# Folding one column of a projection into the stage beside it, and a margin in a list scheduler: a four-layer graph network on one core

## The chip, the cores and the metric

The kernel runs on one core of a Trainium2 chip. The metric is device time in microseconds (us) of one execution; lower is better. Engines are named as in the profile: PE is TensorE (PEld its weight loads), DVE is VectorE, ACT is ScalarE, POOL is GpSimd, SP issues DMAs.

## What is computed

Inputs are `x` (64 graphs, 256 nodes, 128 features, float32) and one weighted adjacency `adj` (256 x 256). Four layers follow each other, each a layer norm, a relu and a graph block whose output is added to `x`:

```
h = relu(layernorm(x)); x = x + GRU(h, adj)          # 5 gated steps, each mixing nodes with adj
h = relu(layernorm(x)); x = x + cheb(h, adj)         # relu([h, A h, 2 A A h - h] @ Theta + bias)
h = relu(layernorm(x)); x = x + conv(h, adj)         # row-normalised ((A h + h) @ W + bias)
h = relu(layernorm(x)); x = x + attention(h, adj)
```

In the attention block, with `W = adj` (256 x 256) cut into two halves of 128 columns, and `E = 256` features:

```
s1 = x @ W[:, :F].T ; s2 = x @ W[:, F:].T            # [B, 256, 256]
pre[i, j, e] = s1[i, e] + s2[j, e] + b_lin[e]
score[i, j] = sum_e leaky_relu(pre[i, j, e]) * a[e] + bias[i, j]
out = sigmoid(softmax_j(score) @ x)
```

The sum over `e` for every pair (i, j) is by far the largest part: 64 x 256 x 256 x 256 elements pass through a min or a relu.

## The kernel before, in words

**Pairs.** Two graphs make a pair; 32 pairs are worked on one after the other. A *front* (`front(p)`) computes the first three layers of pair p and the operands of its attention. *Tiles* make the pairwise elements, *scores* add them up on PE, and a *tail* (`tail`) does softmax, the weighted sum and the store for 128 nodes i of the pair.

**Tiles.** The features are sorted by the sign of `a`, so that two features of equal sign share one pass. A pair has 64 slots of two halves. A relu tile `rl` is 128 x 2048 float32 and belongs to one half of one slot: DVE makes it with one `min` (L854), ACT with eight relu activations (L868), POOL with eight min operations (L876). Three of ten slots are joined: POOL issues a DMA that adds one tile onto the other (L893), so PE sees one tile for two. Thirteen tile buffers circulate; a buffer comes free when PE has scored it or when the DMA has landed.

**Scores.** For a tile PE issues four matmuls of 128x32 weights by 512 columns into one bank (L935), side by side in the four column groups of the array (`side_by_side`, L395 to L398).

**The odd feature.** When one feature has no partner, its contribution is computed apart. In the front, after hT is made, `g2` (128x32; its column 0 gives the linear term, column 1 the s2 term of the odd feature, the rest is zero) is multiplied with four quarters of hT, 128 tokens each, into four partition groups of one bank (L686). Between these, hT's quarter itself is the stationary operand and `w1_odd` (one column) the moving one (L688): that gives the odd feature's s1 with tokens on partitions. ACT copies the bank to `quarter` (L692) and adds the bias into `s1o` (L694). Two DMAs write rows 0 and 1 of each partition group to DRAM (`row`, L699), and one reads them back, broadcast to all partitions (`rows`, L702). The tail uses them at L739 (DVE, with `s1o` as pointer scalar) and L749 (POOL).

**Order.** The order of every engine's instructions is fixed when the kernel is built. A planner keeps a clock for each engine. Fronts, tails and constants are generators which yield the engine of their next step and the time at which its operands are ready; `ran(engine, us, *after)` books the step with a cost written into the code (`PROJECT, MIX, TURN, ...` at L448; 0.6 for the odd stage on PE). `chain_ready(key, e)` returns when a chain's next step may start on an engine. Of what is ready, tails come before fronts, and fronts before tiles and scores; on PE, scores come first when at most one tile buffer is free. Fronts start up to two pairs ahead and are held back by a due count (`STEPS_OF_FRONT`, `SPREAD`, `AHEAD`). Dependencies keep each engine in this order. The planner's times never reach the chip: only the order does, and each engine waits for what an instruction really needs.

The chain of a gated step: mix (PE) -> copy mT (ACT) -> two products (PE) -> tanh (ACT) -> rh (DVE) -> products (PE) -> tanh d (ACT, L561) -> subtract (POOL, L565) -> L568, L572 (DVE, makes hT) -> turn (PE, L426: four 128x128 transposes) -> copy h (ACT, L584) -> the next mix.

Of the kernel before, what the change touches and what calls it, by code (L numbers as in the profile page):

```python
# [8 lines left out]
F32 = mybir.dt.float32  # L9
AF = mybir.ActivationFunctionType  # L10
OP = mybir.AluOpType
# [3 lines left out]
P = 128  # L15
NB = 2
# [6 lines left out]
PE, DVE, ACT, POOL = ENGINES = (mybir.EngineType.PE, mybir.EngineType.DVE, mybir.EngineType.Activation, mybir.EngineType.Pool)  # L23
SLOTS = 64
SHARE = (3, 10)
AHEAD_OF = 2
LOW = 1
ISSUE, ADDED, LANDED, SLACK = 0.65, 5.3, 6.6, 0.3


@with_exitstack
def kernel(
# [50 lines left out]
    nc = tc.nc  # L83
    B, N, D = x.shape
    NC = N // P
    NPAIR = B // NB
# [3 lines left out]
    const = ctx.enter_context(tc.tile_pool(name="const", bufs=1))  # L90
    work = ctx.enter_context(tc.tile_pool(name="work", bufs=2))
# [14 lines left out]
    def ran(engine, us, *after):  # L106
        start = max(clock[engine], 0.0, *after)
        if engine == ACT:
            behind[0] = max(0.0, behind[0] - (start - clock[ACT])) + 0.024 * us
        clock[engine] = start + us  # L110
        return clock[engine] + SEEN[engine] + (behind[0] if engine == ACT else 0.0)

    def moved(since):

        queue[0] = max(queue[0], since) + 0.5
        return queue[0] + 2.2

    spare = [[b, 0.0] for b in banks[5:]]

    def take():  # L120

        spare.sort(key=lambda b: b[1])
        return spare.pop(0)
# [86 lines left out]
    win_n = const.tile([P, 63], F32, name="win_n")  # L210
    w1 = const.tile([P, N], F32, name="w1")
    w2n = const.tile([P, N], F32, name="w2n")
    odd_one = const.tile([P, 34], F32, name="odd_one")
    g2, w1_odd, b_odd = odd_one[:, 0:32], odd_one[:, 32:33], odd_one[:, 33:34]
    blin_s = const.tile([P, NE], F32, name="blin_s")
    SET_UP = set()

# [44 lines left out]
    def other_constants():  # L262
# [5 lines left out]
        t = ran(DVE, 0.8)  # L268

        for c in range(NC):  # L270
            yield PE, t, 1
            b = take()
            for k in range(NC):
                nc.tensor.matmul(b[0][:, 0:N], adj_t[:, k, c * P:(c + 1) * P], adj_n[:, k, :], start=(k == 0), stop=(k == NC - 1))
            t = ran(PE, 1.2, t, b[1])
            yield DVE, t
            nc.vector.tensor_scalar(adj_2[:, c, :], b[0][:, 0:N], 2.0, None, op0=OP.mult)
            t = ran(DVE, 0.35, t)
# [22 lines left out]
        t = ran(DVE, 1.5)  # L301
        yield PE, t, 1
        b = take()
# [5 lines left out]
        t = ran(PE, 0.6, t, b[1])  # L309
        yield DVE, t  # L310
        nc.vector.tensor_copy(columns(14, 3), b[0][:, 0:3])
        t = ran(DVE, 0.1, t)
# [27 lines left out]
        t = ran(DVE, 1.6)  # L340
# [11 lines left out]
        for c in range(NC):  # L352
            yield PE, t, 1
            b = take()
            for k in range(NE):
                nc.tensor.matmul(b[0][:, 0:N], adj_s[:, k, c * P:(c + 1) * P], moved_to[:, k].rearrange("p h m -> p (h m)"),
                                 start=(k == 0), stop=(k == NE - 1))
            t = ran(PE, 1.2, t, b[1])
# [5 lines left out]
            t = ran(DVE, 0.35, t)  # L364
# [3 lines left out]
        b = take()  # L368
# [8 lines left out]
        t = ran(PE, 1.4, t_in, b[1])  # L377
        yield DVE, t
        nc.vector.tensor_copy(blin_s, b[0][:, 1:4:2])
        nc.vector.tensor_copy(odd_one, b[0][:, 4:38])  # L380
        nc.vector.memset(win, 0.0)
        nc.vector.memset(win_n, 0.0)
        nc.vector.tensor_copy(win[:, 31:32], b[0][:, 0:1])
        nc.vector.tensor_scalar(win_n[:, 31:32], b[0][:, 0:1], -1.0, None, op0=OP.mult)
        t = ran(DVE, 0.7, t)
        spare.append([b[0], t])
        SET_UP.add("all")

# [11 lines left out]
    def flat(t):  # L400
        return t.rearrange("p b n -> p (b n)")
# [43 lines left out]
    SHORT = dict(tag="short", bufs=12)  # L445


    PROJECT, MIX, TURN, PRODUCT, PRODUCTS = 0.86, 1.74, 0.69, 0.88, 2.64  # L448
    COPY, BIASED, TANH, ELEMENTS = 0.48, 0.58, 0.57, 0.61

    def norm(src, since, h):

        stats = work.tile([P, NB * NC, 3], F32, name="stats")
        mv = work.tile([P, NB * NC, 2], F32, name="mv")
        s, h = rows_of(src), rows_of(h)[:, :, 0:D]
        yield DVE, since
        for k in range(0, NB * NC, 2):
            nc.vector.bn_stats(stats[:, k:k + 2, :].rearrange("p k s -> p (k s)"), s[:, k:k + 2, :].rearrange("p k d -> p d k"))
        t = ran(DVE, 0.8, since)
        yield POOL, t  # L460
        inverse_root(mv[:, :, 1], stats[:, :, 2], 1.0 / D, OP.mult, LN_EPS, OP.add)
        t = ran(POOL, 1.45, t)
        yield DVE, t
        nc.vector.scalar_tensor_tensor(mv[:, :, 0], stats[:, :, 1], -1.0, mv[:, :, 1], op0=OP.mult, op1=OP.mult)  # L464
        t = ran(DVE, 0.1, t)
        yield ACT, t
        for k in range(NB * NC):
            nc.scalar.activation(h[:, k, :], s[:, k, :], AF.Relu, bias=mv[:, k, 0:1], scale=mv[:, k, 1:2])  # L468
        return ran(ACT, 1.55, t)

    def copied(name, bank, t):

        c = feat(name, **(SHORT if name not in KEPT else KEPT[name]))
        nc.scalar.copy(c, by_feature(bank[0]))  # L474
        t = ran(ACT, COPY, t)
        spare.append([bank[0], t])
        return c, t
# [5 lines left out]
    def front(p):  # L483
# [8 lines left out]
        t = yield from norm(x0, 20.0 if p else 3.0, h)  # L492
        yield PE, t, 1
        b = take()
        to_feature(b[0], h)
        t_h = t
        t = ran(PE, TURN, t, b[1])
        yield ACT, t
        hT, t_hT = copied("hT", b, t)
        for step in range(STEPS):  # L500
            yield PE, t_h, 1, lambda: "adj" in SET_UP
            b = take()
            mix_nodes(b[0], h, adj_t)
            t = ran(PE, MIX, t_h, b[1])
            yield ACT, t
            mT, t_m = copied("mT", b, t)
            if p == 0:
# [6 lines left out]
                t = ran(PE, PROJECT, t_m)  # L514
# [3 lines left out]
            else:  # L518
# [4 lines left out]
                t = ran(PE, 2 * PROJECT, t_m, t_hT, pr[1])  # L523
# [3 lines left out]
            t = ran(ACT, TANH, t, r[1])  # L527
# [4 lines left out]
            if p == 0:  # L532
# [5 lines left out]
                t = ran(PE, PROJECT, t_rh)  # L538
            else:
# [7 lines left out]
                t = ran(PE, 2 * PROJECT, t_rh, pv[1])  # L547
# [6 lines left out]
            if p < 1:  # L554
                nc.scalar.activation(pv[0], pv[0], AF.Tanh, bias=bh, scale=1.0)
                t = ran(ACT, TANH, t)
                yield DVE, t
                nc.vector.tensor_sub(d, by_feature(pv[0]), hT)
                t = ran(DVE, ELEMENTS, t)
            else:  # L560
                nc.scalar.activation(d, by_feature(pv[0]), AF.Tanh, bias=bh, scale=1.0)  # L561
                t = ran(ACT, TANH, t)
# [3 lines left out]
                t = ran(POOL, 1.3, t)  # L566
            yield DVE, max(t, t_z)
            nc.vector.scalar_tensor_tensor(by_feature(pr[0]), by_feature(pr[0]), 1.0, d, op0=OP.add, op1=OP.mult)  # L568
            t = ran(DVE, ELEMENTS, t, t_z)
# [3 lines left out]
            hT = hT_new  # L573
            t_hT = ran(DVE, ELEMENTS)
# [3 lines left out]
            b = take()  # L578
            to_token(b[0], hT)
            t = ran(PE, TURN, t_hT, b[1])  # L580
# [9 lines left out]
        t = ran(DVE, ELEMENTS, t)  # L590
# [6 lines left out]
        b = take()  # L597
        mix_nodes(b[0], h, adj_n)
        t = ran(PE, MIX, t_h, b[1])
# [3 lines left out]
        b = take()  # L603
        to_feature(b[0], h)
        t = ran(PE, TURN, t_h, b[1])
        yield ACT, t
        hT, t = copied("hT", b, t)
        yield PE, t_h, 1
        b = take()
        mix_nodes(b[0], h, adj_2)  # L610
        t = ran(PE, MIX, t_h, b[1])
        yield ACT, t
        c2T, t = copied("c2T", b, t)
# [3 lines left out]
        t = ran(PE, PRODUCTS, t, po[1])  # L617
# [3 lines left out]
        t = ran(DVE, ELEMENTS, t)  # L621
# [3 lines left out]
        t = ran(DVE, ELEMENTS)  # L625
# [4 lines left out]
        t = yield from norm(x2, t, h)  # L630
        yield PE, t, 1
        b = take()
        mix_nodes(b[0], h, adj_ti)
        t = ran(PE, MIX, t, b[1])
        yield ACT, t
        yT, t = copied("yT", b, t)
# [3 lines left out]
        t = ran(PE, PRODUCT, t, po[1])  # L640
# [3 lines left out]
        t = ran(DVE, ELEMENTS, t)  # L644
# [3 lines left out]
        t = ran(ACT, COPY, t)  # L648
# [3 lines left out]
        t = ran(DVE, ELEMENTS, t)  # L652
        yield POOL, t
        inverse_root(rn, rn, MOST_POSITIVE, OP.min, NORM_EPS * NORM_EPS, OP.max)
        t = ran(POOL, 1.35, t)
# [3 lines left out]
        for k in range(NB * NC):  # L659
            nc.vector.scalar_tensor_tensor(rows_of(x3)[:, k], pt[:, k], rn[:, k:k + 1], rows_of(x2)[:, k],  # L660
                                           op0=OP.mult, op1=OP.add)
        t = ran(DVE, 1.04, t)
# [5 lines left out]
        t = yield from norm(x3, t, h3)  # L668
        yield PE, t, 1
        b = take()  # L670
        to_feature(b[0], h3)
        t = ran(PE, TURN, t, b[1])
        yield ACT, t
        hT, t_hT = copied("hT3", b, t)
# [7 lines left out]
        t_s2a = ran(ACT, COPY, t_s2a)  # L682
        yield PE, t_hT, 1
        b = take()
        for g in range(4):
            nc.tensor.matmul(b[0][g * 32:(g + 1) * 32, 0:P], g2, flat(hT)[:, g * P:(g + 1) * P],  # L686
                             start=True, stop=True, skip_group_check=True)
            nc.tensor.matmul(b[0][:, P + g:P + g + 1], flat(hT)[:, g * P:(g + 1) * P], w1_odd, start=True, stop=True)  # L688
        t = ran(PE, 0.6, t_hT, b[1])
        yield ACT, t  # L690
        quarter = work.tile([P, P], F32, name="quarter", bufs=1)
        nc.scalar.copy(quarter, b[0][:, 0:P])  # L692
        s1o = work.tile([P, NB * NC], F32, name="s1o")
        nc.scalar.activation(s1o, b[0][:, P:P + NB * NC], AF.Identity, bias=b_odd, scale=1.0)  # L694
        t = ran(ACT, 0.35, t)
        spare.append([b[0], t])
        row = dram.tile([2, NB * N], F32, name="row", bufs=2)
        for k in range(2):
            nc.sync.dma_start(row[k].rearrange("(q n) -> q n", q=4), quarter[k:P:32, :])  # L699
            t = moved(t) if k else max(t, moved(t) - 2.2)  # L700
        rows = work.tile([P, 2, NB, N], F32, name="rows")
        nc.sync.dma_start(rows.rearrange("p k b n -> p (k b n)"), row.rearrange("k t -> (k t)").unsqueeze(0).to_broadcast([P, 2 * NB * N]))  # L702
# [1 line left out]
        t = moved(t) + 1.5  # L704
        t_lin = t
        yield PE, t_hT, 1
        b = take()
        project(b[0], w2n[:, P:2 * P], hT)
        t = ran(PE, PROJECT, t_hT, b[1])
# [3 lines left out]
        b = take()  # L713
        project(b[0], w1[:, P:2 * P], hT)
        t = ran(PE, PROJECT, t_hT, b[1])
# [6 lines left out]
        b = take()  # L722
        project(b[0], w1[:, 0:P], hT)
        t = ran(PE, PROJECT, t_hT, b[1])
# [235 lines left out]
    def chain_ready(key, e):  # L960

        engine, since, bank, gate = (*CHAINS[key][1], 0, None)[:4] if len(CHAINS[key][1]) < 4 else CHAINS[key][1]
        if engine != e or bank and not spare or gate and not gate():
            return None
        if not isinstance(key, tuple) and 0 < key < NPAIR and spare:

            due = STEPS_OF_FRONT * (scored[0] / (2 * SLOTS) - (key - 2)) / SPREAD
            if CHAINS[key][2] > due + AHEAD:
                return None
        return max(since, min(b[1] for b in spare)) if bank else since  # L970

    def advance(key):
        chain = CHAINS[key]
# [12 lines left out]
    while scored[0] < 2 * NSLOT or CHAINS:  # L986
        while begun_fronts[0] < NPAIR and begun_fronts[0] < 2 + (scored[0] + 2 * SLOTS - 1) // (2 * SLOTS):
            begin_front()
        e = min(now, key=now.get)
        todo = []  # L990
        for key in CHAINS:
            since = chain_ready(key, e)
# [6 lines left out]
        else:  # L999
            since = tile_ready(e)  # L1000
# [6 lines left out]
        if ready:  # L1007
            if e == PE and len(tiles) <= LOW:
                ready = [x for x in ready if x[1] == (2,)] or ready
# [45 lines left out]
```

## Time and profile before

| what | us |
|---|---|
| median of three runs (lowest, highest) | 4951.56 (4950.31, 4957.7) |
| the profiled execution | 4965.92 |
| its span | 4964.1 |
| L854 DVE tiles, 1813 | 4057.4 busy |
| L868 ACT tile parts, 10128 | 4045.6 busy |
| L876 POOL tile parts, 6256 and 1880 | 2962.8 and 899.2 busy |
| L893 POOL issues of adding DMAs, 614 | 575.6 busy |
| L935 PE scores, 27856 records | 2198.3 and 1322.4 busy |
| L686 and L688 PE, 256 records each | 52.1 and 49.8 busy |
| granted PE clock, mean | 0.993 of full speed |

How to read it: a matmul of float32 leaves two records. Matmuls are pipelined, so the distance between the starts of groups, not the length of a record, is what a group costs PE; a score group of eight records starts every 0.86 us. The first 125 us hold the constants and the fronts of pairs 0 and 1; the last front ends at about 4791 us, and from there the engines drain.

### The profile page before, as it was taken

To read this page: it belongs to the slowest core of one execution; us is meant where nothing else is said; L and a number is where in the kernel's file an instruction comes from. 1 tells how busy PE (TensorE), PEld (TensorE's weight loads), DVE (VectorE), ACT (ScalarE), POOL (GpSimd) and SP (SyncE) were. 2 spreads that over 40 slices of the span, in tenths; PEclk is the share of its full clock that TensorE was granted. 3 is DMA by queue.
4 is the path that set the end of the run, shared out by engine and by line. 5 is a ranking of instruction groups with operands and counts; after the bars stand their busy time and mean duration, and the time that the engine had idled before them with its cause. 6 is when DMAs were issued, how large, how long until landed. Compare 5 with 4: busy or idle time off the path is not lost.

```text
span 4964.1 us, 133991 instructions
## 1 busy us (share of the span) xinstructions
PE 4840.3 (98%) x52487; PEld 1793.6 (36%) x52487; DVE 4663.4 (94%) x3288; ACT 4672.1 (94%) x12177; POOL 4684.9 (94%) x9454
## 2 busy tenths in 40 slices
PE   8999999999999999999999999999999999999987
PEld 3333333333333333333333333333333333333322
DVE  3899999999999999999999999999999999999998
ACT  3999999999999999999999999999999999999998
POOL 1899999999999999999999999999999999999998
PEclk9999999999999999999999999999999999999999
DMA  0577667667667676666776676767667767767677
GB/s 18 115 149 145 140 137 148 138 144 150 131 140 147 138 152 138 142 139 135 151 146 139 142 144 132 145 143 144 137 140 145 145 137 143 144 132 144 142 155 145
DMA packets 132363, 687.44 MB, mean 138 GB/s; under 512 B 14096, under 2 KB 49040, under 8 KB 53136
## 3 DMA queue, kind: packets, MB, share of 16 engines
q0 software_dynamic: 88416, 643.86, 64.7%
q1 hardware_dynamic: 42592, 35.01, 2.4%
q8 instruction: 410, 6.72, 0.5%
q14 instruction: 225, 1.84, 0.1%
q10 hardware_dynamic: 720, 0.00, 0.0%
HBM read 26.48 MB, written 8.52 MB: 7 GB/s over the span
## 4 chain that ended last, share of the span: by engine, by line
PE 58%; POOL 11%; DVE 8%; DMA 4%; ACT 4%; issue 3%; POOLq 0%; DVEq 0%; ACTq 0%
PE bank L935 36%; PE bank L398 18%; POOL rl L876 8%; DVE rl L854 6%; DMA rl<-rl 4%; ACT rl L868 3%; PE bank L426 2%; POOL rl L893 1%; PE bank L688 1%; PE bank L686 1%; PE bank L419 1%; POOL d L565 1%; DVE mv L464 0%; POOL mv L393 0%; DVE hT L572 0%
## 5 line engine op out<-in xcount | busy, mean ns | idle before, releaser
L854 DVE TENSOR_TENSOR rl<-s1a,bank 128x2048 f32<-128x2048 f32 x1813 | 4057.4, 2278 | 132.2 <-PE bank L935 70.2
L868 ACT ACTIVATE rl<-bank,s1b 128x256 f32<-128x256 f32 x10128 | 4045.6, 773 | 98.6 <-PE bank L935 57.6
L876 POOL TENSOR_SCALAR rl<-s2n,s1b 128x256 f32<-128x256 f32 x6256 | 2962.8, 669 | 65.0 <-PE bank L935 21.4
L935 PE MATMUL bank<-rl,win_n 128*32 128x512 f32 x17728 | 2198.3, 595 | 56.6 <-DVE rl L854 29.7
L935 PE MATMUL bank<-rl,win 128*32 128x512 f32 x10128 | 1322.4, 594 | 0.0
L935 PEld LDWEIGHTS bank<-rl,win_n 128*32 128x32 f32 x17728 | 555.1, 110 | 1220.6 <-issue 984.5
L876 POOL TENSOR_SCALAR rl<-s2c,s1a 128x256 f32<-128x256 f32 x1880 | 899.2, 658 | 13.6 <-PE bank L935 5.2
L893 POOL DMA_DIRECT2D rl<-rl x614 | 575.6, 949 | 12.5 <-DVE rl L854 6.8
L935 PEld LDWEIGHTS bank<-rl,win 128*32 128x32 f32 x10128 | 324.2, 110 | 653.4 <-issue 535.8
L398 PE MATMUL bank<-mT,wts 128*32 128x512 f32 x2560 | 337.3, 596 | 1.2 <-DVE rh L530 1.1
L398 PE MATMUL bank<-adj_t,h 128*32 128x256 f32 x5120 | 311.8, 383 | 4.8 <-ACT h L584 4.8
L565 POOL TENSOR_TENSOR d<-d,hT 128x512 f32<-128x512 f32 x155 | 227.3, 1466 | 70.0 <-ACT d L561 69.9
L398 PEld LDWEIGHTS bank<-adj_t,h 128*32 128x32 f32 x5120 | 167.8, 111 | 179.2 <-issue 62.1
L468 ACT ACTIVATE h<-x,mv 128x128 f32<-128x128 f32 x384 | 184.2, 766 | 17.3 <-DVE mv L464 16.9
L398 PE MATMUL bank<-hT,wts 128*32 128x512 f32 x1280 | 169.6, 597 | 0.0
L398 PE MATMUL bank<-mT,w 128*32 128x512 f32 x1280 | 168.4, 595 | 0.0
L398 PE MATMUL bank<-rh,u5t 128*32 128x512 f32 x1280 | 167.4, 592 | 0.0
L474 ACT COPY mT<-bank 128x512 f32<-128x512 f32 x160 | 130.4, 815 | 29.9 <-PE bank L398 25.2
L561 ACT ACTIVATE d<-bank,gate_b 128x512 f32<-128x512 f32 x155 | 146.4, 944 | 8.7 <-PE bank L398 8.6
L398 PEld LDWEIGHTS bank<-mT,wts 128*32 128x32 f32 x2560 | 83.5, 110 | 195.5 <-issue 150.8
L526 ACT ACTIVATE bank<-bank,gate_b 128x512 f32<-128x512 f32 x160 | 135.5, 847 | 18.8 <-PE bank L398 18.7
L549 ACT ACTIVATE bank<-bank,gate_b 128x512 f32<-128x512 f32 x160 | 144.2, 901 | 8.8 <-PE bank L398 8.5
(166 smaller groups left out, 3501.6 us busy)
## 6 DMA issues: line engine op xcount, KB each, us to landing
rl<-rl POOLq DMA_DIRECT2D x614, 1024.0 KB, 7.9
rows<-row SPq DMA_DIRECT2D x32, 512.0 KB
xin<-in_x_dram SPq DMA_DIRECT2D x64, 128.0 KB
out_dram<-o SPq DMA_DIRECT2D x64, 128.0 KB
row<-quarter SPq DMA_DIRECT2D x64, 2.0 KB
w_raw<-in_L_gnn_w_w_dram SPq DMA_DIRECT2D x3, 128.0 KB
th_raw<-in_L_gnn_Theta_dram SPq DMA_DIRECT2D x1, 320.0 KB
adj_n<-in_adj_dram SPq DMA_DIRECT2D x1, 256.0 KB
```

The costliest lines, as they stand in the source:

```text
L398: nc.tensor.matmul(o[g:g + 32], w[:, g:g + 32], t, start=start, stop=stop, skip_group_check=True)
L468: nc.scalar.activation(h[:, k, :], s[:, k, :], AF.Relu, bias=mv[:, k, 0:1], scale=mv[:, k, 1:2])
L474: nc.scalar.copy(c, by_feature(bank[0]))
L526: nc.scalar.activation(r[0], pr[0], AF.Tanh, bias=br, scale=0.5)
L549: nc.scalar.activation(pr[0], pr[0], AF.Tanh, bias=bz, scale=0.5)
L561: nc.scalar.activation(d, by_feature(pv[0]), AF.Tanh, bias=bh, scale=1.0)
L565: nc.gpsimd.tensor_sub(d, d, hT)
L854: nc.vector.tensor_tensor(t, rows.to_broadcast(whole), ops["s2a"].unsqueeze(1).to_broadcast(whole), op=OP.min)
L868: nc.scalar.activation(t[:, g, b, :], s2p[:, b, :], AF.Relu, bias=ops["s1"][1][:, b, i:i + 1], scale=-1.0)
L876: nc.gpsimd.tensor_scalar(t[:, part, b, :], ops["s2n" if k else "s2c"][:, b, :], ops["s1"][min(k, 1)][:, b, row], MOST_NEGATIVE, op0=OP.mi ...
L893: nc.gpsimd.dma_start(out=t.rearrange("p g b n -> p (g b n)"), in_=z.rearrange("p g b n -> p (g b n)"), accum_op=OP.add)
L935: nc.tensor.matmul(pe[g * 32:(g + 1) * 32, :], w[:, 31 - r:63 - r], flat(t[:, g]), start=False, stop=(left[block] == 0), skip_group_check= ...
```

## The change

Three things are edited. The column `w1_odd` becomes column 2 of the 32-column operand `g2`, so that the four matmuls of L686 also give the odd feature's s1, as a third row of each partition group; the four matmuls with hT as stationary operand go. To bring this row to partitions, the tokens of each matmul are no longer 128 consecutive ones: group g takes runs of 32 tokens, 128 apart, and DVE transposes `quarter` in blocks of 32 x 32, whose columns 2, 34, 66 and 98 then hold the four node blocks; the bias is added there by DVE, not by ACT. The two row DMAs use runs of 32 values accordingly. The planner's costs for these steps follow (PE 0.35 for 0.6, ACT 0.3 for 0.35, DVE 0.4 new). Apart from that, the planner's cost of a turn rises from 0.69 to 0.80, and `chain_ready` adds `SURE` (0.6 us) to the ready time of every step on PE of the fronts 1 to 31.

```diff
+SURE = 0.6
...
-    odd_one = const.tile([P, 34], F32, name="odd_one")
-    g2, w1_odd, b_odd = odd_one[:, 0:32], odd_one[:, 32:33], odd_one[:, 33:34]
+    odd_one = const.tile([P, 33], F32, name="odd_one")
+    g2, b_odd = odd_one[:, 0:32], odd_one[:, 32:33]
...
-        nc.vector.tensor_copy(odd_one, b[0][:, 4:38])
+        nc.vector.tensor_copy(odd_one[:, 0:32], b[0][:, 4:36])
+        nc.vector.tensor_copy(odd_one[:, 2:3], b[0][:, 36:37])
+        nc.vector.tensor_copy(b_odd, b[0][:, 37:38])
...
-    PROJECT, MIX, TURN, PRODUCT, PRODUCTS = 0.86, 1.74, 0.69, 0.88, 2.64
+    PROJECT, MIX, TURN, PRODUCT, PRODUCTS = 0.86, 1.74, 0.80, 0.88, 2.64
...
+        tokens = flat(hT).rearrange("p (q g i) -> p q g i", g=4, i=32)
         for g in range(4):
-            nc.tensor.matmul(b[0][g * 32:(g + 1) * 32, 0:P], g2, flat(hT)[:, g * P:(g + 1) * P],
-                             start=True, stop=True, skip_group_check=True)
-            nc.tensor.matmul(b[0][:, P + g:P + g + 1], flat(hT)[:, g * P:(g + 1) * P], w1_odd, start=True, stop=True)
-        t = ran(PE, 0.6, t_hT, b[1])
+            nc.tensor.matmul(b[0][g * 32:(g + 1) * 32, 0:P], g2, tokens[:, :, g, :], start=True, stop=True, skip_group_check=True)
+        t = ran(PE, 0.35, t_hT, b[1])
         yield ACT, t
         quarter = work.tile([P, P], F32, name="quarter", bufs=1)
         nc.scalar.copy(quarter, b[0][:, 0:P])
+        t = ran(ACT, 0.3, t)
+        spare.append([b[0], t])
+        yield DVE, t
+        turned = work.tile([P, P], F32, name="turned", bufs=1)
+        nc.vector.transpose(turned, quarter)
         s1o = work.tile([P, NB * NC], F32, name="s1o")
-        nc.scalar.activation(s1o, b[0][:, P:P + NB * NC], AF.Identity, bias=b_odd, scale=1.0)
-        t = ran(ACT, 0.35, t)
-        spare.append([b[0], t])
+        nc.vector.tensor_scalar(s1o, turned[:, 2:P:32], b_odd, None, op0=OP.add)
+        ran(DVE, 0.4, t)
         row = dram.tile([2, NB * N], F32, name="row", bufs=2)
         for k in range(2):
-            nc.sync.dma_start(row[k].rearrange("(q n) -> q n", q=4), quarter[k:P:32, :])
+            nc.sync.dma_start(row[k].rearrange("(q g i) -> g q i", g=4, i=32), quarter[k:P:32, :].rearrange("g (q i) -> g q i", i=32))
...
-        return max(since, min(b[1] for b in spare)) if bank else since
+        since = max(since, min(b[1] for b in spare)) if bank else since
+        return since + (SURE if e == PE and isinstance(key, int) and 0 < key < NPAIR else 0.0)
```

More of the change, by code (lines that the diff above doesn't have):

```diff
@@ L384, in other_constants @@
         nc.vector.tensor_scalar(win_n[:, 31:32], b[0][:, 0:1], -1.0, None, op0=OP.mult)
-        t = ran(DVE, 0.7, t)
+        t = ran(DVE, 0.9, t)
         spare.append([b[0], t])
```

## The prediction

> **What bounds the kernel now.** I read the page's first two parts, then the busy time in windows, then who waited for whom, then the timeline around the stage that the change rewrites. The profiled execution took 4965.9 us, of which 4964.1 are span; the median of the runs shown is 4951.6, so this execution is 14 us (0.3%) longer. Savings below are read from the span and taken off the median.
>
> ```profile
> span 4964.1 us, 133991 instructions
> PE 4840.3 (98%) x52487; PEld 1793.6 (36%) x52487; DVE 4663.4 (94%) x3288; ACT 4672.1 (94%) x12177; POOL 4684.9 (94%) x9454
> ...
> PE 58%; POOL 11%; DVE 8%; DMA 4%; ACT 4%; issue 3%; POOLq 0%; DVEq 0%; ACTq 0%
> ```
>
> Averages mix a start-up, where two fronts run alone, and a drain. So I asked for the steady part, 300 to 4700 us; the columns of this answer are microseconds of window, then busy time (and instructions) of PE, weight loads, DVE, ACT, POOL:
>
> ```profile
> sum 4400.00, PE 4350.72 PEld 1618.27 DVE 4222.79 ACT 4223.03 POOL 4272.14; mean PE 870.14 PEld 323.65 DVE 844.56 ACT 844.61 POOL 854.43
> ```
>
> PE is busy 98.9%, POOL 97.1%, DVE and ACT 96.0%. All four are near full, with PE nearest. Idle: PE 49 us, POOL 128, DVE and ACT 177 each. The waits of that window say who holds whom:
>
> ```profile
> DVE rl L854 <- PE bank L935: 66.2, 107, 2.0
> ...
> ACT rl L868 <- PE bank L935: 57.3, 77, 2.7
> ...
> POOL rl L876 <- PE bank L935: 23.9, 29, 2.4
> POOL rl L876 <- DMA rl<-rl: 16.6, 19, 2.0
> ...
> PE bank L426 <- DVE hT L572: 16.6, 18, 2.8
> PE bank L935 <- DMA rl<-rl: 8.6, 11, 2.4
> PE bank L935 <- DVE rl L854: 6.0, 8, 1.7
> ```
>
> The three makers of relu tiles wait for PE to give tiles back; PE waits for them 15 us in 4400, and 33 us at steps of fronts (turn L426 21, L419 4, products of L398 8). PE bounds this kernel, POOL closely behind it.
>
> **A rule of the skill against the trace.** The Trainium skill, "TensorEngine Tiling (Array Packing)", section Key Properties, says that column tiles work independently and in parallel, but that changing the tiling mode drains the engine. The stage at L686 and L688 alternates the two modes:
>
> ```profile
> 2049.51 0.38 PE L686 MATMUL bank<-hT,odd_one 128*32 128x128 f32 x2
> 2049.82 0.38 PE L688 MATMUL bank<-odd_one,hT 128*128 128x1 f32 x2
> 2050.13 0.41 PE L686 MATMUL bank<-hT,odd_one 128*32 128x128 f32 x2
> ...
> 2051.77 0.38 PE L688 MATMUL bank<-odd_one,hT 128*128 128x1 f32 x2
> 2052.08 1.07 PE L935 MATMUL bank<-rl,win_n 128*32 128x512 f32 x8
> ```
>
> From 2049.51 to 2052.08 the stage holds PE for 2.57 us, four times 0.64, although each single matmul has at most 128 columns. The nearest unmixed row is the projection of yT: 32 records of 128x32 by 128 columns run from 2015.59 to 2016.46, 0.87 us, so 8 records cost 0.22. The trace agrees with the rule, and the forecast goes by these two durations. The planner books 0.6 us for this stage, so PE runs about 2 us behind its plan once a front.
>
> **The change, part by part.**
>
> *Removed on PE.* Four matmuls of L688 (each with a 128x128 weight load) go, and the four of L686 then stand alone. 2.57 becomes 0.22: 2.35 us per front. No row shows a moving operand cut into runs of 32 values 128 apart. Bounds: as dense, 0.22; twice that plus one mode change's worth of delay (half of 0.64), 0.76. I take 0.22, since the transposes and L935 show no cost of layout that I could price. 32 fronts have the stage; the last runs at 4781 us, where PE is busy only 173 of 200 us, so 31 count: 73 us (56 at the other bound). Front 0's is on the path to the first tile (DVE waited 14.1 us for s1a there), so it counts.
>
> *Moved from ACT to DVE.* ACT loses the 128x4 activation (32 x 0.34 = 11 us); DVE gains a 32x32-block transpose of 128x128 and a 128x4 add with a pointer. The skill, "VectorE: DVE Perf Modes", section The three transpose paths, gives 0.31 us for 128x128 in bf16; no run here shows f32. The trace's DVE rows of 128x128 f32 take 0.29 (L244) and a 128x256 copy 0.42 (L227); I take 0.30, bounds 0.29 and 0.42. The add: 0.16 (L326) to 0.37 (L464). Together 0.46 x 32 = 15 us, range 14 to 25. The three setup copies add 2 x 0.16 once, nothing. Behind these two on DVE stands the next relu tile; but s1o is first read by the pair's first tail, about 100 us later, so nobody waits for them.
>
> *Row DMAs.* Each of the 64 writes keeps its 2 KB and its place on SP's queue; it becomes 16 pieces of 128 bytes instead of 4 of 512. The write now takes 2.8 us of SP's waiting on average (26 waits, 71.7 us). Were it 2 us longer, rows would still land some 90 us before the tail reads it (front 0: issued at 131, first used at 223.5). What waits on SP behind it is out and x traffic with tens of us of room. Nothing, while that cover stands.
>
> *Plan.* TURN 0.80 for 0.69 and SURE 0.6 change no instruction, only order. A turn costs 0.70 by the timeline (2047.93 to 2048.63), so the new figure is a little cautious. I compared the two programs' instruction orders. Work by engine: DVE makes 7 more tiles (7 x 2.24 = 16 us), ACT 40 fewer activations (40 x 0.38 = 15), POOL 16 fewer operations (16 x 0.455 = 7); the number of joined pairs, 614, stays. So DVE +31, ACT -26, POOL -7. On PE, counted in pitch time, the distance from a mix to the product that reads its copy grows from 7.4 to 7.9 us, from a turn to the next mix from 2.8 to 3.4; from the candidate product (rh,u5t) to the turn that waits for hT it is 10.7 before and 10.3 after. So the costliest stall, L426's, gets no more cover in the order, and I book nothing of the 33 us; it could be up to 20. Fronts finish later: the PE work between a pair's last projection and its first tile falls from 29.4 to 25.5 us on average, and for pair 26 to zero. That one pair may stop POOL for 3 us.
>
> *Who takes up the 73 us.* POOL can't run faster than its own work. Its 128 us of idle hold 27 for PE (24 at tiles, 3 at a tail) and 17 for DMA; the rest is waits inside chains and gaps between instructions. With those 44 gone and its work 7 less, the span can shrink 51 before POOL is as full as its other waits allow. DVE has 66 + 13 for PE and 38 for DMA, less 31 of new work: 86. ACT has some 100 for PE. So POOL cuts the gain at 51; less the 3 at pair 26: **48 us, 4904**.
>
> **Rivals.**
> 1. *PE goes on holding* (it would show POOL at 98.5% and more): 73 us, and up to 20 of the stalls at fronts: 4860 to 4880. For it: POOL's chain waits may shrink as PE keeps to its plan. Against: POOL has nothing near 1.5% of slack that the waits explain.
> 2. *The makers hold earlier.* DMA waits stay (the additions' landing takes 7.9 us where the plan books 6.6), POOL gives 27 + 7 = 34, and DVE's extra work collides: 10 to 35 us, 4917 to 4941, middle 4927.
> 3. *The plan is reshuffled and the gain goes in new waits*: stalls at L935 and L426 as large as what is freed; within 10 us, about 4950.
> 4. *Slower: late fronts.* A front has 31 steps on PE; each booked 0.6 later makes 19 us if all are felt. The lead of 25 us then vanishes in most pairs, and every maker stops at a pair's start. Priced at 4 us for 20 pairs, 80 us against 51: 4981. It decides from 51/20 = 2.6 us per late pair. Against it: the order shows only one pair at zero, the next shortest leads 15 us and more.
>
> **How the numbers follow.** Forecast (35 to 70 us gained) 0.55; rival 1, 0.15; rival 2, 0.18; rival 3, 0.06; rival 4, 0.06. 0.2% of the median is 10 us, about what a measurement of this kernel can tell from no change. Faster 0.88, same 0.06, slower 0.06. The range leaves out the lower half of rival 1 and rivals 3 and 4: 4864 to 4938.
>
> **What would show it.** Right: no L688-like row; the stage's four matmuls about 0.22 apart from the next group's start; PE's busy time down by some 60 to 75 us; waits on L935 by DVE, ACT and POOL well under 66, 57 and 24; POOL at 98% in the steady part. Wrong: the stage at 0.7 us (strided operand or mode change); waits of DVE or POOL on s1a or s1b at pair starts (rival 4); PE idle in the steady part over 100 us with L426 and L935 waiting for DVE, which would say that the order, not the work, sets the time.

## The result and the profile after

Fifteen runs of each kernel side by side: 4963.4 us (4951.8 to 4968.2) for the changed kernel, 4952.5 us (4948.6 to 4960.4) for the kernel before; ratio 1.0018, interval [1.0011, 1.0025]. It is 0.2% slower, where 1% faster was forecast. The profiled execution of the changed kernel took 4957.3 us, 6 us less than its median, and that of the kernel before 13 us more than its own; so the two spans below stand in the wrong order, and shares and waits are read from them, not the difference.

Line numbers move by a few with the change: L854 (DVE's tiles), L868 (ACT's), L876 (POOL's), L893 (joins), L935 (scores), L426 (turn) and L464 are L860, L874, L882, L899, L941, L429 and L467 in the changed kernel, and a few lines off these in the variants.

The first lines of the page after, and the busy time of PE, weight loads, DVE, ACT and POOL from 300 to 4700 us (read the sums; the means are per stretch of the query):

```profile
span 4955.5 us, 133351 instructions
PE 4781.3 (96%) x52231; PEld 1745.2 (35%) x52231; DVE 4713.3 (95%) x3361; ACT 4641.4 (94%) x12105; POOL 4658.7 (94%) x9438
...
PE 33%; POOL 16%; DVE 13%; ACT 6%; DMA 6%; issue 4%; POOLq 0%; DVEq 0%; ACTq 0%
```

```profile
sum 4400.00, PE 4300.48 PEld 1574.29 DVE 4273.10 ACT 4195.40 POOL 4251.86; mean PE 860.10 PEld 314.86 DVE 854.62 ACT 839.08 POOL 850.37
```

PE lost 59 us of busy time, at the lower edge of the 60 to 75 that were forecast, and its share of the chain that ended last fell from 58% to 33%; POOL and DVE took its place there. In the steady part PE went from 98.9% busy to 97.7%: the freed time became idle. DVE went from 96.0% to 97.1% (50 us more in 4400), while ACT and POOL fell, to 95.4% and 96.6%. PE's part of the stage is as forecast; the timeline:

```profile
2052.77 0.40 PE L690 MATMUL bank<-hT,odd_one 128*32 128x128 f32 x8
2052.99 1.04 PE L941 MATMUL bank<-rl,win_n 128*32 128x512 f32 x8
```

0.22 us from start to start, where it was 2.57. The waits of the makers and of PE in the steady part (total, times, longest):

```profile
DVE rl L860 <- DMA rl<-rl: 48.2, 44, 3.2
...
DVE rl L860 <- PE bank L941: 16.2, 25, 2.2
```

```profile
POOL rl L899 <- DVE rl L860: 18.5, 15, 2.2
POOL rl L882 <- PE bank L941: 18.4, 16, 3.3
POOL rl L882 <- DMA rl<-rl: 14.7, 15, 3.2
```

```profile
PE bank L429 <- DVE hT L575: 36.3, 35, 4.7
PE bank L941 <- DMA rl<-rl: 21.0, 20, 4.0
PE bank L941 <- DVE rl L860: 16.2, 17, 5.7
```

Over all three makers, waits of tiles on PE fell from 147 to 79 us, and tiles' waits on the adding DMA rose from 88 to 111. PE's own waits, all added up, rose from 48 to 98 us, about as much as its busy time fell in this window (50). Who waited for whom turned round: PE now waits for hT (17 before, 36 after), for the DMA (9, 21) and for DVE's tiles (6, 16), although a margin had been put on just those steps. And one group stands out among DVE's; columns: line, engine, operation, shapes, count, then busy us and mean ns, then idle us of the engine just before:

```profile
L701 DVE TENSOR_SCALAR s1o<-turned,odd_one 128x4 f32<-128x4 f32 x32 | 40.3, 1260 | 1.1
...
L699 DVE STREAM_TRANSPOSE turned<-quarter 128x128 f32<-128x128 f32 x32 | 9.8, 305 | 6.1 <-ACT quarter L694 6.1
```

The transpose costs 0.305 us, as taken. The add of four values costs 1.26 us on average (minimum 0.229, median 0.481, longest record 5.9), against 0.16 taken and 0.37 as the upper bound.

### The profile page after: what moved, and what is told of

Its sections match the earlier page's. It is cut to its first block, busy times and chain, and to the rows that moved or that the text cites. A ratio compares the mean times of both kernels' runs of the same rounds, so it can differ in the third digit from the quotient of the medians.

```text
span 4955.5 us, 133351 instructions
## 1 busy us (share of the span) xinstructions
PE 4781.3 (96%) x52231; PEld 1745.2 (35%) x52231; DVE 4713.3 (95%) x3361; ACT 4641.4 (94%) x12105; POOL 4658.7 (94%) x9438
## 4 chain that ended last, share of the span: by engine, by line
PE 33%; POOL 16%; DVE 13%; ACT 6%; DMA 6%; issue 4%; POOLq 0%; DVEq 0%; ACTq 0%
PE bank L941 21%; POOL rl L882 13%; PE bank L401 11%; DVE rl L860 10%; DMA rl<-rl 6%; ACT rl L874 5%; POOL rl L899 1%; PE bank L429 1%; POOL d L568 1%; POOL mv L396 0%; PE bank L422 0%; DVE hT L575 0%; DVE bank L571 0%; DVE mv L467 0%; POOL sc L755 0%
## 5 line engine op out<-in xcount | busy, mean ns | idle before, releaser
L860 DVE TENSOR_TENSOR rl<-s1a,bank 128x2048 f32<-128x2048 f32 x1820 | 4070.5, 2280 | 73.2 <-DMA rl<-rl 48.2
L874 ACT ACTIVATE rl<-bank,s1b 128x256 f32<-128x256 f32 x10088 | 4034.5, 811 | 107.8 <-DMA rl<-rl 51.9
L882 POOL TENSOR_SCALAR rl<-s2n,s1b 128x256 f32<-128x256 f32 x6296 | 2965.4, 667 | 55.6 <-PE bank L941 15.6
L941 PE MATMUL bank<-rl,win_n 128*32 128x512 f32 x17768 | 2216.6, 595 | 79.4 <-DVE rl L860 42.4
L941 PE MATMUL bank<-rl,win 128*32 128x512 f32 x10088 | 1321.2, 594 | 0.0
L941 PEld LDWEIGHTS bank<-rl,win_n 128*32 128x32 f32 x17768 | 559.8, 110 | 1270.9 <-issue 956.0
L882 POOL TENSOR_SCALAR rl<-s2c,s1a 128x256 f32<-128x256 f32 x1824 | 872.7, 674 | 6.8 <-PE bank L941 2.8
L899 POOL DMA_DIRECT2D rl<-rl x614 | 576.7, 947 | 40.5 <-DVE rl L860 21.7
L941 PEld LDWEIGHTS bank<-rl,win 128*32 128x32 f32 x10088 | 325.7, 110 | 631.8 <-issue 506.4
L429 PE MATMUL bank<-ident,hT 128*128 128x128 f32 x640 | 107.1, 291 | 48.5 <-DVE hT L575 45.2
```

Source lines behind the costliest of these rows:

```text
L429: nc.tensor.transpose(pt[:, b, c, :], ht[:, b, c * P:(c + 1) * P], ident)
L860: nc.vector.tensor_tensor(t, rows.to_broadcast(whole), ops["s2a"].unsqueeze(1).to_broadcast(whole), op=OP.min)
L874: nc.scalar.activation(t[:, g, b, :], s2p[:, b, :], AF.Relu, bias=ops["s1"][1][:, b, i:i + 1], scale=-1.0)
L882: nc.gpsimd.tensor_scalar(t[:, part, b, :], ops["s2n" if k else "s2c"][:, b, :], ops["s1"][min(k, 1)][:, b, row], MOST_NEGATIVE, op0=OP.mi ...
L899: nc.gpsimd.dma_start(out=t.rearrange("p g b n -> p (g b n)"), in_=z.rearrange("p g b n -> p (g b n)"), accum_op=OP.add)
L941: nc.tensor.matmul(pe[g * 32:(g + 1) * 32, :], w[:, 31 - r:63 - r], flat(t[:, g]), start=False, stop=(left[block] == 0), skip_group_check= ...
```

## The experiments

Three theories were put against each other. *Makers*: once PE is relieved, POOL, DVE and ACT hold, so the freed time can't be used. *Port*: the add on DVE waits for POOL and eats the gain. *Order*: the planner's new numbers make a worse order. Ratios are to runs of the kernel before on the same chip (its medians there were 4952 to 4965 us, so times are not compared across batches). The cuts of edits below show the lines that matter.

### What each part does

**no_add.** The order of the changed kernel kept, the add on DVE gone:

```diff
-        nc.vector.tensor_copy(b_odd, b[0][:, 37:38])
+        nc.vector.tensor_reduce(b_odd, ident[:, 2:P:32], AX.X, OP.add)
+        nc.vector.tensor_mul(b_odd, b_odd, b[0][:, 37:38])
...
-        nc.scalar.copy(quarter, b[0][:, 0:P])
+        nc.scalar.activation(quarter, b[0][:, 0:P], AF.Identity, bias=b_odd, scale=1.0)
...
-        nc.vector.tensor_scalar(s1o, turned[:, 2:P:32], b_odd, None, op0=OP.add)
+        s1o = turned[:, 2:P:32]
```

> The changed kernel with its order kept, but the odd feature's bias is added by ACT's copy into quarter (a per-partition bias that is zero except on row 2 of each group), so that DVE's add at L701 (40.3 us, mean 1.26 us, longest 5.9) is gone. Port theory (that add waits inside itself for POOL, and what it holds up on DVE is what ate the gain): 35 to 40 us less DVE time, 4925 to 4935. Makers theory (POOL, ACT and DVE are full together, one engine's relief is little): 4950 to 4958. Order theory (the new order costs): at most 10 us, 4953.

Measured 0.9980 [0.9972, 0.9988], against 1.0018 with the add: 0.38%, some 19 us. The add is a cause, about half as dear as its theory said, and not the only one. A second pair says the same in another order: no_add_old_plan (0.9950, below) is rows_only (0.9994, below) without the add, 0.44% apart.

**add_two_inputs.** Same order, the add in another form:

```diff
-        nc.vector.tensor_scalar(s1o, turned[:, 2:P:32], b_odd, None, op0=OP.add)
+        nc.vector.tensor_tensor(s1o, turned[:, 2:P:32], b_odd.to_broadcast([P, NB * NC]), op=OP.add)
```

> The changed kernel, order kept, with L701's add as a tensor_tensor of two SBUF operands (the bias broadcast) in place of tensor_scalar with a pointer. If only the one-input form waits for POOL: about 0.16 us each, and the time of no_add, ratio 0.997 to 0.999. If two inputs in SBUF wait as well: a mean near 1.2 us and the time of the changed kernel, 1.000 to 1.003.

1.0023 [1.0015, 1.0032], the time of the changed kernel. Its group:

```profile
L701 DVE TENSOR_TENSOR s1o<-turned,odd_one 128x4 f32<-128x4 f32 x32 | 32.1, 1002 | 1.1
```

The form hardly matters; both wait. A stretch of the changed kernel's timeline shows what runs beside such a wait:

```profile
697.45 6.45 POOL L882 TENSOR_SCALAR rl<-s2n,s1b 128x256 f32<-128x256 f32 x14
...
700.36 0.30 DVE L699 STREAM_TRANSPOSE turned<-quarter 128x128 f32<-128x128 f32 x1
...
700.70 5.92 DVE L701 TENSOR_SCALAR s1o<-turned,odd_one 128x4 f32<-128x4 f32 x1
...
703.69 1.04 POOL L899 DMA_DIRECT2D rl<-rl  x1
...
704.05 8.87 DVE L860 TENSOR_TENSOR rl<-s1a,bank 128x2048 f32<-128x2048 f32 x4
```

POOL runs 14 operations without a gap from 697.45 to 703.90. The transpose passes beside them in 0.30 us; the add, started at 700.70, lets DVE go on only at 704.05, when POOL's row has ended (the record of 5.92 us reaches past that and overstates the hold of 3.35). A row's end is not what frees the add in general: nine of the 32 adds hold DVE for over 1 us, and in at least five of them DVE goes on while POOL's row runs on. The longest started at 993.73 and held 5.69 us, inside 16 operations from 992.63 to 999.87. What ends a hold stays open.

The Trainium skill, "SBUF — State Buffer", section Who interferes with whom, has a rule that fits: VectorE and GpSimd share one pair of ports under an exclusive lock, which a tensor_scalar with one SBUF input can take, and a DVE instruction with two SBUF inputs contends with GpSimd's reads as well. Both forms waited here. By the same section the loser waits until the instruction that holds the pair is done; measured, the hold of 3.35 us spans some seven of POOL's operations (one starts every 0.45 us), so the price comes from the measurement and not from the length of one operation. No run here shows the ports themselves. The large tiles at L860 read one operand from PSUM; they show a mean of 2.28 us and a maximum of 2.57, so no such hold. A form of the add that does not wait beside POOL was not run; no_add takes out its plain work, at least 0.23 us each or 7 us in all, together with its waits.

**rows_only and plan_only.** The change cut in two: `SURE = 0.0` and `TURN = 0.69` in the changed kernel; `SURE = 0.6` and `TURN = 0.80` in the kernel before.

> The third row alone, with the turn's cost back at 0.69 and no margin on PE steps of fronts. Order theory (margin and turn cost move fronts and tiles so that new waits arise): 30 to 50 us faster than the changed kernel, 4915 to 4935. Makers theory: within 12 us of the changed kernel, 4950 to 4970. Port theory: the add still waits, within 12 us of the changed kernel.

> The kernel before with the planner's two numbers of the change (turn 0.80, margin 0.6), all work as before. Order theory: 30 to 60 us slower than before, 4985 to 5010, since PE has all its work and the order is the worse one. Makers theory: within 15 us of before, since only the order moves. A helpful margin: PE's 33 us of waits at front steps halve, 4935 to 4945.

0.9994 [0.9986, 1.0002] and 0.9996 [0.9988, 1.0004]. The planner's numbers alone change nothing that can be told; the third row with its add and its own plan entries, but without the numbers, changes nothing either. Without the numbers the changed kernel is 0.24% better. PE's waits for hT did fall with the margin (55 us in rows_only, 36 in the changed kernel) and the time still rose: those waits are not what sets the end.

**work_only.** The work of the third row with every engine's order as before: the planner's costs untouched, the bias in ACT's copy as in no_add, the transpose put behind s1a without a step of its own.

```diff
         t_n = ran(ACT, BIASED, t)
         spare.append([b[0], t_n])
+        turned = work.tile([P, P], F32, name="turned")
+        nc.vector.transpose(turned, quarter)
+        s1o = turned[:, 2:P:32]
```

> Every engine's order as in the kernel before; only the odd feature's work is changed (third row, four matmuls gone, 2.35 us of PE per front; the bias in ACT's copy; one transpose on DVE after the last projection). Order theory and port theory: the freed PE time shows, 4895 to 4915. Makers theory: PE becomes idle instead, DVE, ACT and POOL stay where they are, 4935 to 4955; their waits on PE at L935 shrink, and waits on the adding DMA or on each other take their place.

0.9937 [0.9924, 0.9949]: 31 us faster, between the two expectations. In the steady part (busy times, then POOL's longest waits):

```profile
sum 4400.00, PE 4311.99 PEld 1580.09 DVE 4247.67 ACT 4247.28 POOL 4299.75; mean PE 4311.99 PEld 1580.09 DVE 4247.67 ACT 4247.28 POOL 4299.75
```

```profile
POOL rl L879 <- DMA rl<-rl: 16.5, 21, 2.2
POOL mv L395 <- DVE stats L461: 8.6, 5, 5.9
POOL rl L879 <- PE bank L938: 7.5, 7, 2.2
```

POOL is 97.7% busy; its busy time per 4400 us rose from 4272 to 4300, by 0.65%, which is the gain. So its idle fell by 28 us, from 128 to 100: its tile waits on PE from 24 to 7.5, its waits at steps of fronts and tails from 22 to 13, while those on the DMA stayed (16.6, 16.5). PE's idle grew from 49 to 88.

### Who holds: PE, POOL, or both

**pe_relief** takes another 56 us from PE, **pool_relief** 90 us from POOL, both on work_only's order; **pool_relief_before** takes the same from POOL in the kernel before. What each leaves out is in its expectation.

```diff
-            for b in range(NB):
-                side_by_side(by_feature(pe)[:, b, :], ident, adj_n[:, ic, :], b == 0, False)
...
-                             start=False, stop=(left[block] == 0), skip_group_check=True)
+                             start=first, stop=(left[block] == 0), skip_group_check=True)
```

```diff
-            nc.gpsimd.tensor_add(sc, sc, ops["lin"])
```

> Work_only with 512 more matmuls of PE left out of the computation: the 64 groups that put the adjacency into the score bank (64 x 0.87 = 56 us), order kept. If PE still held a part: another 20 to 40 us, ratio 0.986 to 0.990. If PE no longer holds after the third row and the makers or chains do: within 10 us of work_only, ratio 0.992 to 0.996, and PE idle in the steady part up by some 45 us.

> Work_only (the order of before, third row, no add on DVE) with POOL's addition of the linear term in 63 tails left out of the computation (63 x 1.4 = 90 us of POOL, nothing else moved). If POOL is what holds after PE is relieved: 25 to 60 us faster than work_only, ratio to before 0.982 to 0.989. If the order's chains hold (PE waits for hT, makers for the adding DMA): within 12 us of work_only, ratio 0.991 to 0.996.

> The kernel before, its order kept, with POOL's addition of the linear term in 63 tails left out of the computation (90 us of POOL); the odd stage as before. If PE alone held before (the forecast's reading): within 10 us of before, ratio 0.998 to 1.000. If POOL and PE held together: 20 to 50 us faster, 0.990 to 0.996, less than the 65 us that the same relief gave once PE was relieved.

| | POOL as it was | POOL relieved by 90 us |
|---|---|---|
| PE as before | 1 | 0.9938 [0.9926, 0.9950] |
| PE relieved by the third row | 0.9937 [0.9924, 0.9949] | 0.9806 [0.9794, 0.9819] |

pe_relief stands at 0.9926 [0.9912, 0.9940], not to be told from work_only. Each relief alone gives 0.6%, PE's for some 75 us taken off, POOL's for 90; both give 1.9%, more than the sum. Once PE is relieved, more relief of PE gives nothing that can be told, and POOL's gives 65 us, a little more than the 25 to 60 expected. So in the kernel before the two held together. That either alone soon meets the other, POOL's side shows: in pool_relief_before PE is busy 99.4%, and the makers' tile waits on PE are 190 us, where they were 147.

```profile
sum 4400.00, PE 4375.22 PEld 1631.55 DVE 4250.48 ACT 4259.75 POOL 4234.28; mean PE 4375.22 PEld 1631.55 DVE 4250.48 ACT 4259.75 POOL 4234.28
```

A shorter tail is no rival for the gain: in the kernel before, DVE's maximum over the scores (nmx, L753) waited only 4 us in all for the addition that was left out. With both relieved PE is busy 98.8%:

```profile
sum 4400.00, PE 4346.80 PEld 1601.36 DVE 4301.31 ACT 4288.78 POOL 4262.88; mean PE 4346.80 PEld 1601.36 DVE 4301.31 ACT 4288.78 POOL 4262.88
```

### Order

**no_add_old_plan** is no_add without margin and with the turn at 0.69; it differs from work_only only by order. **margin_only** is no_add with the turn at 0.69.

> No_add with the turn at 0.69 and no margin: third row, bias in ACT's copy, the stage's new costs and its own DVE step in the plan. It differs from work_only only by order. If margin and turn cost are what took no_add from work_only (0.998 against 0.9937): back to 0.993 to 0.995. If it is the stage's own entries in the plan (lower PE cost, one more paced step, so fronts finish 2 to 6 us of PE work later): 0.997 to 1.000.

> No_add with the turn's cost back at 0.69 and the margin kept at 0.6; no_add itself stood at 0.998 and without both numbers at 0.995. If the margin is what costs: 0.997 to 1.000. If the turn's cost is: 0.994 to 0.996. The order of this one finishes fronts latest (four pairs with at most 0.6 us of PE work between last projection and first tile), so late fronts as a cause would show as makers waiting for s1a or s1b at pair starts, and a ratio above 0.999.

0.9950 [0.9937, 0.9963] and 1.0000 [0.9992, 1.0008]. With the third row and no add, the margin costs 0.5% by itself, and 0.3% together with the turn's cost (no_add). In margin_only the makers' waits at steps of fronts and tails (not at tiles) sum to 274 us in 4400, against 139 in no_add_old_plan. Its order has the latest fronts, so lateness was the next theory. It was tried by letting fronts run six steps further ahead, in these three:

```diff
-    STEPS_OF_FRONT, SPREAD, AHEAD = 109, 1.7, 2
+    STEPS_OF_FRONT, SPREAD, AHEAD = 109, 1.7, 8
```

> No_add_old_plan with AHEAD 8 for 2, so fronts may run six steps further ahead; the lead rises from 23 to 40 us of PE work, and no pair is below 32. If late fronts cost: the 0.13% against work_only comes back, 0.992 to 0.994. If lateness costs nothing: 0.995 to 0.998, since work piles up at the other end.

> Margin_only with AHEAD 8 for 2: mean lead 21 to 27, but five pairs stay at or below 1 us, so those fronts are limited by their own length and not by the due count. Late fronts as the cause: it stays within 0.2% of margin_only, 0.998 to 1.001, and 0.5% above early_fronts. Margin harmful by order alone: it shifts as early_fronts shifts against no_add_old_plan.

> No_add (margin and turn 0.80) with AHEAD 8: mean lead 32, two pairs at zero, the next at 9. Late fronts as the cause: between the other two, 0.995 to 0.997, better than no_add's 0.998. Margin by itself: no better than 0.998.

early_fronts 1.0006 [0.9998, 1.0015], early_fronts_margin 0.9999 [0.9990, 1.0007], early_fronts_both 1.0034 [1.0021, 1.0046]. The first misses both of its expectations, and the second is not 0.5% above the first, as late fronts would have it. The theory falls: the kernel whose fronts are earliest lost 0.56% against no_add_old_plan. DVE's tiles waited for s1a at most 11 us in 4400 in any of these. So orders of nearly the same work spread from 0.9937 to 1.0034, and neither lead nor margin sorts them. What comes nearer to sorting them is the makers' waits at steps of fronts and tails, here of the seven kernels with the third row and no add:

| | ratio | those waits, us in 4400 |
|---|---|---|
| work_only | 0.9937 | 117 |
| no_add_old_plan | 0.9950 | 139 |
| no_add | 0.9980 | 170 |
| early_fronts | 1.0006 | 219 |
| early_fronts_both | 1.0034 | 234 |
| early_fronts_margin | 0.9999 | 252 |
| margin_only | 1.0000 | 274 |

The last two break the row, and a wait is a sign, not its reason. Why one order is good stays open.

The granted PE clock was not held equal in these comparisons. In each batch of the kernel before, an execution with a mean clock lower by 0.001 took 3.4 to 3.8 us longer. The means of the other kernels lie between 0.9925 and 0.9962, but rows_only's 13 runs stand at 0.9908, against 0.9934 for the kernel before beside it; by that slope, an estimate, 9 us of its time would go with the clock. For the add (no_add at 0.9940, the changed kernel at 0.9926) it would be 5 of the 19 us. Whether an order brings its clock with it, no run shows, so differences of 0.1 to 0.2% between orders are not settled.

### Versions that might beat both

**fewer_joins** is work_only planned anew with `SHARE = (27, 100)`. **lin_on_pe** is work_only planned anew with the linear term added by PE in the score bank, POOL's addition gone:

```diff
+        if left[block] == 0:
+            for b in range(NB):
+                side_by_side(by_feature(pe)[:, b, :], share, READY[p]["lin"][:, b, :], False, False)
+            ran(PE, 0.87, since, READY[p]["t_lin"])
```

> Work_only's kernel planned anew with 27 of 100 slots joined, not 30: 552 adding DMAs for 614, so PE gets 62 more scores (53 us), POOL 62 fewer issues (58 us, part of it filled with tiles again), and fewer waits for the adding DMA. If the makers hold: 10 to 30 us faster than work_only, ratio 0.988 to 0.992. If PE holds again: 0.996 to 1.002.

> Work_only planned anew, with the linear term added in the score bank by PE (eight matmuls a block of a constant 1/128 with the broadcast row, 64 x 0.87 = 56 us of PE) in place of POOL's addition (90 us). If POOL holds, as pool_relief says: 20 to 40 us faster than work_only, ratio 0.985 to 0.990. If PE holds again with 56 us more: 0.993 to 1.000.

0.9936 [0.9924, 0.9948] and 0.9928 [0.9916, 0.9941]. The first lies between its two expectations, the second just under its second one; neither gave 20 us more than work_only. Work moved from POOL to PE meets PE again (lin_on_pe: PE back at 98.9% busy, makers' tile waits on PE back at 163 us). lin_on_pe, 0.7% faster than the kernel before, and work_only, which is the third row without its planner's numbers and without the add, beat both kernels.

## Why the prediction was wrong, point by point

In microseconds of the median: the forecast's gain of 48 was 31 for the work alone, and three terms booked at nothing or near it took from that 6 (the stage's entries in the plan), 15 (margin and turn) and 19 (the add), which leaves a loss of 9.

- *PE bounds this kernel, POOL closely behind it.* Half right. The reading of busy shares (98.9 and 97.1%) was right; that PE is the bound and POOL comes behind it was not: POOL relieved alone by 90 us gives as much (0.9938) as PE relieved alone by some 75 (0.9937), so the two held together.
- *Removed on PE, 2.35 us per front.* Right: 2.57 became 0.22, busy time fell by 59 us. That the change of mode was what cost is not shown by it: each step of L688 before took 0.31 us, of which its two weight loads, gone with it, took 0.30:

```profile
2049.82 0.30 PEld L688 LDWEIGHTS bank<-odd_one,hT 128*128 128x128 f32 x2 [0.20 <-issue]
```

- *POOL cuts the gain at 51.* The mechanism was right and the size too large: work_only, the change without add and reordering, gained 31. The term mis-sized is the 44 us of POOL's waits that were all to go: 28 us of idle went. Of 24 at tiles for PE 16 went, the 17 for the DMA stayed at 16.5, as rival 2 said; the waits inside chains, left out of the sum, gave 9.
- *The add, 0.16 to 0.37, and nobody waits for it.* Wrong, and it cost 0.38% (no_add against the changed kernel), because what stands behind it on DVE waited: nine adds held DVE for over 1 us. The price was taken from an idle set-up (L326) and a mean (L464). The row that warned was in the trace before, whose columns here are minimum, median and maximum in ns:

```profile
L464 DVE SCALAR_TENSOR_TENSOR mv<-stats,mv x128: 140/165/6962, 5.8 to 4765.5; 128x4 f32<-128x4 f32 x128
```

  A mean of 368 beside a median of 165 and a maximum of 6962, on an instruction of four values with two SBUF inputs, is a wait inside the record: at the longest one, started at 4231.34, DVE's next instruction starts 6.88 us later, with POOL at work all the time. "Behind these two stands the next relu tile" was seen; what that tile would pay was not.
- *SURE and TURN change only order; I book nothing.* Nothing was right for the work of before (plan_only 0.9996), wrong beside the third row: 0.30% without the add (no_add against no_add_old_plan), 0.24% with it (the changed kernel against rows_only). Why the order costs stays open.
- *The stage's own entries in the plan* (its lower cost, one more step) went unpriced: 0.9950 against 0.9937, 0.13%, hardly beyond the intervals.
- The sum in ratios: -0.63% work, +0.13% entries, +0.30% margin and turn, +0.38% add: +0.18%, the measured sum; it closes by construction, since each term is the difference of two kernels in this order. Taken the other way round, add first, the last two are +0.44% and +0.24%.
- *Rival 3* (the gain goes in new waits) named the outcome at 0.06, and its sign came: PE's waits grew by 50 us where its busy time fell by 50. It did not name the add. *Rival 4*'s price fell: fronts came late and no tile of the changed kernel waited for s1a or s1b in the steady part.
- *The signs.* Of the makers' waits on the scores only DVE's fell far (66 to 16; ACT 57 to 40, POOL 24 to 18), and POOL stood at 96.6%, not 98. The sign for "the order sets the time", over 100 us of idle PE with turn and scores waiting for DVE, was met but for half a microsecond: 99.5 us.

## What to carry to other kernels

When four engines are all above 95% busy, the fullest is not "the bound": take a gain on it as capped by the next one's real slack, and count of that slack first the waits on the relieved engine: here these gave 16 of 28 us, waits on the DMA nothing. Before a small instruction is put on an engine, look at the spread of its like in the trace, not at its mean: a median far below the mean, as 165 ns beside 368 here, can say that it waits inside its record, and then everything queued behind it pays. And when a list scheduler is run again with new costs, keep one build in which the order is held fixed; without it, 0.5% of reshuffling can't be told from the change.

## What the runs showed of the hardware

- A DVE operation of 128x4 values, both operands in SBUF, took 0.23 us at its fastest and 1.26 us on average as a tensor_scalar beside POOL's back-to-back operations, 0.16 and 1.00 us with two SBUF inputs; single ones held DVE for up to 5.7 us. A 32x32-block transpose of 128x128 f32 took 0.298 to 0.311 us in all 32 cases beside the same POOL work.
- Matmuls that alternate between 32-column tiles and the whole array cost 0.64 us a pair here, weight loads of 128x128 among it; the four 32-column ones alone cost 0.22 together, with a moving operand cut into runs of 32 values.
